# Row tiles over the score buffers, and a projection bias that is added at the zero frequency

## The chip, the cores and the metric

The kernel runs on one core of one Trainium2 chip. The metric is the device time of one execution in microseconds (us). Before the change it is 3673.48 us, the median of three runs (3665.2 to 3677.16).

## The reference

The input `x` is two images of 48 x 48 positions with 768 channels, float32. Two layers follow one another, each added to its own input:

```
def _L0(x):                     # attention over 2304 tokens, 12 heads of 64
    qkv = x.reshape(B, S, dim) @ qkv_w + qkv_b
    attn = (q * scale) @ k.T + rel_h[..., :, None] + rel_w[..., None, :]
    out = softmax(attn) @ v
    return out @ proj_w + proj_b

def _L1(x):                     # a small network per frequency
    xf = rfft2(x, axes=(1, 2), norm='ortho')
    o1 = gelu(block_diagonal(w1) applied to xf + b1)     # complex
    o2 = softshrink(block_diagonal(w2) applied to o1 + b2, 0.01)
    return irfft2(o2, s=(48, 48), norm='ortho')

x = x + _L0(group_norm(x))      # 32 groups
x = x + _L1(group_norm(x))
```

`proj_b` is one value per channel, the same for all 2304 positions of an image. In the transform over both axes such a constant stands at one frequency alone, the zero frequency, where it is 48 times as large.

## The kernel before

The kernel is written with a tile library. Pools of tiles are stacked from the left or from the right end of the on-chip memory; a pool that is opened where another was closed waits for those that used the old one. The library puts each engine's instructions into an order of its own, except those issued through the class `InOrder`: each of these is pinned behind everything already written on its engine. SP issues most transfers, ACT the stores of `y1` and a few at the end of stages.

**Attention** (`attention`) handles both images, 216 units in a row: 12 pairs of heads (`pr`), six groups of 384 queries (`g`), three units of 128 queries each (`x`). A unit's scores stand in one of four buffers `s` of the pool `at_s` (128 partitions, 18,432 bytes each). POOL fills `s` with the position terms; PE adds products, DVE takes the maximum, ACT the exponential, DVE transposes blocks of 32; then `exchange` brings them into `pT` with 12 transfers and 4 copies by ACT; PE (`weigh`, tile `ps_o`) makes the weighted sum two units later. `x` counts units in the loop by `n`; `e` is `n` counted so that the last unit has 17. The results of a unit's group go to DRAM as `oT`, the inverse denominators as `inv_d`; for the last group ACT issues these stores.

**Projection** (`Projection`, `project_out`): 18 row tiles `t` of 128 tokens, in six groups `g` of three. One product (`product`) is 6 matmuls of 384 columns into a bank `acc`; there are two halves `hf` per tile. `parts` loads the tokens of one group in two halves, then `inv_d` in two halves, and has POOL multiply the two. Image 0's projection (`late`) is begun inside attention: `late.early` loads group 0, and at `e` = 11 to 19 nine `late.step()` load the weights (3), the bias (1) and group 1 (4 loads and POOL's product). `late.fill` puts the first six products between the last units. For image 1 `prepare` does the like during the last stages of image 0's spectral part, in a pool `po_r` (`room`).

The sum `x1` (row tile, [128, 24, 768]) holds image rows two by two: partitions 0 to 47 the even one, 64 to 95 and 112 to 127 the odd one. It is allocated after attention, over attention's closed pools. `rows(g)` (L921) loads four pairs of image rows from `x` by SP, three transfers per group, and for image 0 two more that fill the partitions in between (48 to 63, 96 to 111); then POOL adds the bias in four instructions (L930). `outputs` (L963) adds the products into `x1` on DVE, by the pieces that `moves` (L762) yields: 13 for three row tiles and one half. `over_w(n)` (L938) transforms two pairs of rows over the width: eight matmuls `ps_y` over both halves, four copies `y1` by ACT, and two stores `y_d`.

In the loop over `t`, `tokens(g + 1)` and `rows(g + 1)` stand at the first tile of each group.

**Spectral part** (`Spectral`, eight blocks `n` of 96 channels): `load` reads `y_d`; `weights`, `biases` load by SP; `over_h(n)` transforms over the height (`ps_z`, copies by DVE and ACT in turn, squares by ACT); `mean(n)` subtracts the group's mean at the zero frequency (L1092); `norm(n)` makes the group's root from the squares and scales `w1` (L1118), and has POOL add real and imaginary parts into `both`; `first` and `second` are the two layers; `back_h`, `back_w` transform back and add into `x1`, from where the output is stored.

`mean(0)` and `norm(0)` are called from inside `over_h(1)`. PE takes its instructions in order, so the rest of `over_h(1)` stands behind the products in them.

Of the kernel before, what the change touches and what calls it, by code (L numbers as in the profile page):

```python
# [17 lines left out]
P = 128  # L18
# [24 lines left out]
XP = 8  # L43
WP = 5
# [230 lines left out]
def attention(tc, k, xs, a, oTs, inv_ds, late, span, ps_b, ps_o):  # L275
# [12 lines left out]
    with ExitStack() as ctx:  # L288
# [11 lines left out]
        sp = pool("at_s", 4)  # L300
# [362 lines left out]
        for n in range(len(order) + 3):  # L663
# [110 lines left out]


class Projection:


    def __init__(self, tc, k, a, oT, inv_d, span, ps_b, dram, room=None, first=None):
# [5 lines left out]
        if room is not None:  # L785
            shape = [P, self.head + 2 * NCC * UQ]
# [7 lines left out]
        self.steps = [lambda i=i: self.weights(i) for i in range(0, NCC, 2)] + [self.bias]  # L794
# [28 lines left out]
    def pb(self):  # L823
        at = NCC * C if self.room is None else 2 * NCC * UQ
        return self.fixed()[:, at : at + C]
# [14 lines left out]
    def bias(self):  # L840

        src = self.a["proj_b"] if self.k.pb_d is None else self.k.pb_d
        self.nc.sync.dma_start(out=self.pb, in_=src.partition_broadcast(P))

    def values_bias(self, hf):
# [13 lines left out]
        nc.vector.tensor_tensor(self.pb[:, cols], ps[:, :UQ], self.pb[:, cols], ALU.add)  # L859
        if hf:  # L860
            k.pb_d = self.dram.tile([C], F32, tag="pb_d", name="pb_d")
            nc.sync.dma_start(out=k.pb_d, in_=self.pb[0, :])
# [44 lines left out]

def project_out(tc, k, x_b, pr, pools, y_d, x1, constants):
# [9 lines left out]
    x_v = x_b.rearrange("(g k i w) c -> g i w k c", k=4, i=2, w=HW)  # L918
# [12 lines left out]

    rows(0)
# [588 lines left out]
```

## Time and profile before

The profiled execution took 3675.21 us; its span, from first to last instruction, is 3673.4 us, and the 1.8 us beside it lie around the span.

| engine | busy us | share of the span | instructions |
|---|---|---|---|
| PE (matmul) | 3538.6 | 96% | 36416 |
| PEld (weight load, beside PE) | 2447.8 | 67% | 36416 |
| DVE | 2938.3 | 80% | 6867 |
| ACT | 2552.4 | 69% | 3769 |
| POOL | 2045.6 | 56% | 661 |

The stages, read from the chain of waits in order of time:

| stage | from, us | to, us |
|---|---|---|
| attention, both images | 0 | 2846 |
| projection and width of image 0 | 2846 | 3010 |
| spectral part of image 0 | 3010 | 3259 |
| projection and width of image 1 | 3259 | 3424 |
| spectral part of image 1 | 3424 | 3673 |

A busy share is an average over these stages. The chain is followed back from the last instruction, at each step to what released it; it says what the end waited for, stage by stage. "L67" is the line of `InOrder` and stands for every instruction issued through it, so there the tile names tell the groups apart. An instruction's row names the tiles without their numbers: `x` is `x1`, `s` a score buffer, `proj_s` and `proj` the places of the projection of image 0 and 1, `spectrum` all that is cut from one large tile (`z` of even blocks, `d2` and others). SPq and ACTq are the issuing of transfers.

### The profile page before, as it was taken

To read this page: it belongs to the slowest core of one execution; us is meant where nothing else is said; L and a number is where in the kernel's file an instruction comes from. 1 tells how busy PE (TensorE), PEld (TensorE's weight loads), DVE (VectorE), ACT (ScalarE), POOL (GpSimd) and SP (SyncE) were. 2 spreads that over 40 slices of the span, in tenths; PEclk is the share of its full clock that TensorE was granted. 3 is DMA by queue.
4 is the path that set the end of the run, shared out by engine and by line. 5 is a ranking of instruction groups with operands and counts; after the bars stand their busy time and mean duration, and the time that the engine had idled before them with its cause. 6 is when DMAs were issued, how large, how long until landed. Compare 5 with 4: busy or idle time off the path is not lost.

```text
span 3673.4 us, 93676 instructions
## 1 busy us (share of the span) xinstructions
PE 3538.6 (96%) x36416; PEld 2447.8 (67%) x36416; DVE 2938.3 (80%) x6867; ACT 2552.4 (69%) x3769; POOL 2045.6 (56%) x661
## 2 busy tenths in 40 slices
PE   8999999999999999999999999999888799989998
PEld 5676776767767666676776776767666357645665
DVE  4798989998989996799898998989895456645575
ACT  3788888888888887788888888888885024301342
POOL 2566666666665654557576766676673333434232
PEclk9999999999999999999999999999999899999898
DMA  3677777777777885677777777777887775586545
GB/s 105 148 179 172 175 176 175 172 177 173 181 170 178 209 198 118 141 174 180 171 180 167 181 172 175 178 175 172 185 188 164 158 167 116 138 204 163 119 108 140
DMA packets 499085, 608.09 MB, mean 166 GB/s; under 512 B 179249, under 2 KB 311665, under 8 KB 498642
## 3 DMA queue, kind: packets, MB, share of 16 engines
q1 hardware_dynamic: 489692, 585.36, 69.2%
q10 hardware_dynamic: 8950, 16.72, 1.4%
q8 instruction: 289, 4.73, 0.6%
q14 instruction: 154, 1.26, 0.1%
HBM read 133.77 MB, written 85.90 MB: 60 GB/s over the span
## 4 chain that ended last, share of the span: by engine, by line
PE 85%; DMA 5%; DVE 3%; SPq 2%; ACT 1%; issue 1%; POOL 1%; ACTq 0%; DVEq 0%; POOLq 0%
PE ps_o L67 22%; PE ps_s L67 20%; PE ps_proj L67 15%; PE ps_v L67 8%; PE acc L67 7%; PE ps L1206 4%; DVE s L67 2%; PE ps_z L1145 2%; PE ps_u L1245 2%; SPq L67 2%; PE ps_r L67 2%; DMA pT<-s 1%; PE ps_x L67 1%; PE ps_y L67 1%; POOL s L67 1%
## 5 line engine op out<-in xcount | busy, mean ns | idle before, releaser
L67 POOL TENSOR_TENSOR s<-rhw 128x2304 f32<-128x2304 f32 x432 | 1740.6, 4063 | 1032.3 <-DMA pT<-s 559.6
L67 DVE CUSTOM_DVE_ANT_0 s<-ps_s,s 128x512 f32<-128x512 f32 (+1 forms) x2160 | 1222.1, 633 | 308.4 <-issue 224.7
L67 ACT ACTIVATE s<-s,nm 128x1152 f32<-128x1152 f32 x864 | 1074.7, 1245 | 338.1 <-DVE nm L67 331.5
L67 DVE STREAM_TRANSPOSE s<-s 128x1152 f32<-128x1152 f32 x864 | 1111.9, 1344 | 6.0 <-ACT s L67 6.0
L67 ACT COPY pT<-s 32x1152 f32<-32x1152 f32 x864 | 993.6, 1150 | 28.9 <-PE ps_o L67 10.3
L67 PE MATMUL ps_o<-pT,v 128*64 128x128 f32 x15552 | 904.7, 276 | 46.3 <-DMA pT<-s 17.4
L67 PEld LDWEIGHTS ps_o<-pT,v 128*64 128x64 f32 x15552 | 873.3, 139 | 89.4 <-issue 40.5
L67 PE MATMUL ps_s<-kT,qT 64*128 64x512 f32 (+1 forms) x4320 | 902.6, 555 | 6.3 <-ACT xnT L67 2.7
L67 PEld LDWEIGHTS ps_s<-kT,qT 64*128 64x128 f32 x4320 | 432.7, 186 | 421.5 <-issue 345.2
L67 PE MATMUL ps_proj<-xnT,w 128*64 128x384 f32 (+1 forms) x4032 | 592.5, 447 | 4.1 <-ACT xnT L67 2.9
L67 PEld LDWEIGHTS ps_proj<-xnT,w 128*64 128x64 f32 x4032 | 280.4, 138 | 280.0 <-issue 216.8
L969 DVE TENSOR_TENSOR x<-acc,x 32x384 f32<-32x384 f32 (+2 forms) x312 | 173.0, 554 | 189.8 <-PE acc L67 84.5
L67 PE MATMUL ps_v<-w,xnT 128*64 128x128 f32 x5184 | 298.9, 275 | 0.0
L67 PEld LDWEIGHTS ps_v<-w,xnT 128*64 128x64 f32 x5184 | 283.4, 137 | 21.2 <-DVE mx L67 21.2
L956 ACT COPY y<-ps_y 128x384 f32<-128x384 f32 x96 | 40.1, 489 | 318.7 <-PE ps_y L67 290.4
L67 POOL TENSOR_TENSOR spectrum<-spectrum 128x480 f32<-128x480 f32 x80 | 96.2, 1205 | 200.2 <-DVE nm_total L1103 117.4
L67 DVE DVE_READ_ACCUMULATOR2_ANT mx<- 128x1 f32 x2160 | 179.1, 83 | 0.0
L67 ACT ACTIVATION_READ_ACCUMULATOR s<-s,nm 128x1 f32 x864 | 161.2, 187 | 0.0
L1206 PE MATMUL ps<-w,spectrum 96*64 96x96 f32 x3200 | 141.7, 247 | 0.0
L1206 PEld LDWEIGHTS ps<-w,spectrum 96*64 96x64 f32 x3200 | 133.4, 137 | 7.1 <-DVE spectrum L1222 2.9
L67 PE MATMUL acc<-proj_s 128*128 128x384 f32 x360 | 121.5, 496 | 0.1
L67 PEld LDWEIGHTS acc<-proj_s 128*128 128x128 f32 x360 | 68.5, 193 | 53.6 <-issue 8.2
(138 smaller groups left out, 2227.9 us busy)
## 6 DMA issues: line engine op xcount, KB each, us to landing
pT<-s SPq DMA_DIRECT2D x2592, 144.0 KB
t<-rel SPq DMA_DIRECT2D x144, 189.0 KB
rhw<-t SPq DMA_DIRECT2D x144, 144.0 KB
y<-y_d SPq DMA_DIRECT2D x40, 360.0 KB
u_d<-spectrum SPq DMA_DIRECT2D x40, 360.0 KB
u<-u_d SPq DMA_DIRECT2D x48, 300.0 KB
w<-in_qkv_w SPq DMA_DIRECT2D x36, 384.0 KB
oT<-res SPq DMA_DIRECT2D x71, 192.0 KB
```

What stands on the lines that cost most here:

```text
L67: return lambda *args, **kw: self.tc.keep_in_program_order(op(*args, **kw))
L956: nc.scalar.copy(y1[:, i, cols], both[i][:, :UQ])
L969: nc.vector.tensor_tensor(dst, acc[p : p + n, :UQ], dst, ALU.add)
L1145: nc.tensor.matmul(ps[:BS, w * 96 : (w + 1) * 96], lhsT=self.y2[s, j][:, w, i * BS : (i + 1) * BS], rhs=k.fh, start=True, stop=True,)
L1206: nc.tensor.matmul(ps[64 * r : 64 * r + 64, w * BS : (w + 1) * BS], lhsT=self.o1[:, ri, f0 : f0 + 64], rhs=w2[:, (0, 2, 1, 0)[2 * r + ri], ...
L1245: nc.tensor.matmul(ps[: 2 * HW, :480], lhsT=k.ih, rhs=d2[:, c0 : c0 + 480], start=True, stop=True)
```

## The change

- The pool of the score buffers is opened by the caller, at the right end of the memory. At `e` = 18, when the last unit's exchange has been written, `exchanged()` closes it and opens in its place three row tiles `x1[0..2]` of [128, 8, 768] (together as large as the four buffers), and loads the rows of group 0 there: four transfers on SP, ahead of that step's `late.step()`. The fill of partitions 48 to 63 (`BETWEEN`) comes one group later than the rows. After attention, `project_out` no longer loads group 0 for image 0; `fw` is loaded at the very start of the kernel.
- The rows get no bias. `proj_b` is loaded into one partition, `values_bias` makes one row of it, and `pb_d` keeps it in DRAM. Image 1 has no bias step any more, so its nine steps become eight.
- The spectral part of image 0 loads `pb_d` twice (`dc`, a row of 768; `dc_off`, 96 x 8, by single elements), POOL multiplies both by 48, PE and DVE subtract the group's mean. `mean` adds `dc_off` in the same instruction; `second` adds `dc` to the zero frequency's output with one POOL instruction of 1 x 96 per block.
- `over_w` reads 48 partitions of the even row instead of 64, and `moves` yields 14 pieces instead of 13 for three tiles and one half.

```diff
-def attention(tc, k, xs, a, oTs, inv_ds, late, span, ps_b, ps_o):
+def attention(tc, k, xs, a, oTs, inv_ds, late, exchanged, sp, span, ps_b, ps_o):
-        sp = pool("at_s", 4)
...
-            elif 1 < e < 7:
+            elif e == 18:
+                exchanged()
+            if 1 < e < 7:
                 next(late.early)
             elif 11 <= e < 20:
                 late.step()

 def moves(t):
-    done = 0
+    wide = False
     for p in range(0, P, 32):
         k, m = divmod(t % 3 * 4 + p // 32, 3)
-        if p >= done:
-            n = min(P, p + 96 - 32 * m) - p if p in (0, 64) and m == 0 else 32
-            yield p, n, k, 32 * m
-            done = p + n
-        if m == 1:
+        if m == 0:
+            wide = p in (0, 64)
+            yield p, HW if wide else 32, k, 0
+        elif m == 1:
+            if not wide:
+                yield p, HW - 32, k, 32
             yield p, 32, k, 96
+        else:
+            yield p, 32, k, 64

 class Projection:
...
-        self.steps = [lambda i=i: self.weights(i) for i in range(0, NCC, 2)] + [self.bias]
+        self.steps = [lambda i=i: self.weights(i) for i in range(0, NCC, 2)]
+        if k.pb_d is None:
+            self.steps.append(self.bias)
...
     def bias(self):
-        src = self.a["proj_b"] if self.k.pb_d is None else self.k.pb_d
-        self.nc.sync.dma_start(out=self.pb, in_=src.partition_broadcast(P))
+        self.nc.sync.dma_start(out=self.pb, in_=self.a["proj_b"][None, :])

     def values_bias(self, hf):
...
-                ps[:, :UQ],
-                lhsT=k.bv[:, cc : cc + 1].to_broadcast([P, P]),
+                ps[:1, :UQ],
+                lhsT=k.bv[:, cc : cc + 1],

+ROWS = ((0, 0, 0, HW), (64, 1, 0, 32), (112, 1, 32, 16))
+BESIDE = (96, 0, 32, 16)
+BETWEEN = (HW, 1, 32, 16)
+
+def load_rows(sync, x_b, x1, g, places):
+    x_v = x_b.rearrange("(g k i w) c -> g i w k c", k=4, i=2, w=HW)
+    part = x1[g // 2][:, g % 2 * 4 : g % 2 * 4 + 4, :]
+    for q, i, w0, n in places:
+        sync.dma_start(out=part[q : q + n], in_=x_v[g, i, w0 : w0 + n])

     def rows(g):
-        part = x1[:, 4 * g : 4 * g + 4, :]
-        places = [(0, 0, 0, HW), (64, 1, 0, 32), (112, 1, 32, 16)]
-        if pr.room is None:
-            places += [(HW, 1, 32, 16), (96, 0, 32, 16)]
-        for q, i, w0, n in places:
-            pr.sync.dma_start(out=part[q : q + n], in_=x_v[g, i, w0 : w0 + n])
-        for j in range(4):
-            pr.pool.tensor_tensor(part[:, j, :], part[:, j, :], pr.pb, ALU.add)
-
-    rows(0)
+        fresh = pr.room is None
+        load_rows(pr.sync, x_b, x1, g, (*ROWS, BESIDE) if fresh else ROWS)
+        if fresh:
+            load_rows(pr.sync, x_b, x1, g - 1, (BETWEEN,))
+            if g == HW // 8 - 1:
+                load_rows(pr.sync, x_b, x1, g, (BETWEEN,))
+
+    if pr.room is not None:
+        rows(0)
     constants()
     while pr.steps:
         pr.step()
...
-                    r = slice(64 * i, 64 * i + 64)
+                    r = slice(64 * i, 64 * i + (64 if i else HW))

 class Spectral:
+    def constants_at_zero(self):
+        nc, k = self.nc, self.k
+        if k.dc is not None:
+            return
+        k.dc = self.small.tile([1, C], F32, tag="dc", name="dc")
+        k.dc_off = self.small.tile([BS, NBK], F32, tag="dc_off", name="dc_off")
+        self.sync.dma_start(out=k.dc, in_=k.pb_d[None, :])
+        with nc.allow_non_contiguous_dma(reason="biases onto partitions"):
+            self.sync.dma_start(out=k.dc_off, in_=k.pb_d.rearrange("(n o) -> o n", o=BS))
+        self.pool.tensor_scalar(k.dc, k.dc, float(HW), 0.0, ALU.mult, ALU.add)
+        self.pool.tensor_scalar(k.dc_off, k.dc_off, float(HW), 0.0, ALU.mult, ALU.add)
+
+    def offsets_at_zero(self):
+        nc, off = self.nc, self.k.dc_off
+        mean = self.bank("ps_nm")
+        nc.tensor.matmul(mean[:BS, :NBK], lhsT=self.k.gmean, rhs=off, start=True, stop=True)
+        nc.vector.tensor_tensor(off, off, mean[:BS, :NBK], ALU.subtract)

     def mean(self, n):
...
-        nc.vector.tensor_tensor(z0, z0, mean[:BS, :1], ALU.subtract)
+        nc.vector.scalar_tensor_tensor(
+            z0, z0, self.k.dc_off[:, n : n + 1], mean[:BS, :1], ALU.add, ALU.subtract
+        )

     def second(self, n, ahead):
...
             self.pool.tensor_tensor(val, val, clip, ALU.subtract)
+            if j == 0:
+                dc = self.d2[:1, 0, i * BS : (i + 1) * BS]
+                self.pool.tensor_tensor(dc, dc, k.dc[:, n * BS : (n + 1) * BS], ALU.add)

     def run(self):
...
         self.biases()
+        fresh = k.dc is None
+        self.constants_at_zero()
         over_h(0)
+        if fresh:
+            self.offsets_at_zero()

 def block_kernel(tc, a, out):
-        k.load(nc.sync, a, cp, {"rel": [P, 2 * REL]})
+        k.load(nc.sync, a, cp, {"rel": [P, 2 * REL], "fw": [P, 64]})
...
+        s_rooms, x1 = ExitStack(), [None] * 3
+        in_order = InOrder(tc, nc.sync)
+
+        def exchanged():
+            s_rooms.close()
+            x_pool = ctx.enter_context(tc.tile_pool(name="sp_x", bufs=1, side="right"))
+            for j in X1_ORDER:
+                x1[j] = x_pool.tile([P, XP, C], F32, tag=f"x1_{j}", name=f"x1_{j}")
+            load_rows(in_order, a["x"][0], x1, 0, (*ROWS, BESIDE))
+
+        sp = s_rooms.enter_context(tc.tile_pool(name="at_s", bufs=4, side="right"))
+        attention(tc, k, a["x"], a, oTs, inv_ds, late, exchanged, sp, span, ps_b, ps_o)
```

Every other use of `x1` (`over_w`, `outputs`, `back_w` and its stores) picks the tile and the row in it; `X1_ORDER` is (1, 0, 2).

More of the change, by code (lines that the diff above doesn't have):

```diff
@@ L43 @@
 XP = 8
+X1_ORDER = (1, 0, 2)
 WP = 5
@@ L785, in __init__ @@
         if room is not None:
-            shape = [P, self.head + 2 * NCC * UQ]
+            shape = [P, NCC * C + 2 * NCC * UQ]
             self.room = room.tile(shape, F32, tag="proj", name="proj")
@@ L823, in pb @@
     def pb(self):
-        at = NCC * C if self.room is None else 2 * NCC * UQ
-        return self.fixed()[:, at : at + C]
+        return self.spans()[:1, NCC * C : NCC * C + C]
     def weights(self, c0):
@@ L858, in values_bias @@
             )
-        nc.vector.tensor_tensor(self.pb[:, cols], ps[:, :UQ], self.pb[:, cols], ALU.add)
+        nc.vector.tensor_tensor(self.pb[:, cols], ps[:1, :UQ], self.pb[:, cols], ALU.add)
         if hf:
             k.pb_d = self.dram.tile([C], F32, tag="pb_d", name="pb_d")
-            nc.sync.dma_start(out=k.pb_d, in_=self.pb[0, :])
+            nc.sync.dma_start(out=k.pb_d[None, :], in_=self.pb)
     def product(self, t, hf):
@@ L917, in project_out @@
     bank = lambda name: ps_b.tile([P, 512], F32, tag="b", name=name)
-    x_v = x_b.rearrange("(g k i w) c -> g i w k c", k=4, i=2, w=HW)
     y_v = y_d.rearrange("(q i) t c -> t q i c", i=2)
     def rows(g):
-        part = x1[:, 4 * g : 4 * g + 4, :]
-        places = [(0, 0, 0, HW), (64, 1, 0, 32), (112, 1, 32, 16)]
-        if pr.room is None:
-            places += [(HW, 1, 32, 16), (96, 0, 32, 16)]
-        for q, i, w0, n in places:
-            pr.sync.dma_start(out=part[q : q + n], in_=x_v[g, i, w0 : w0 + n])
-        for j in range(4):
-            pr.pool.tensor_tensor(part[:, j, :], part[:, j, :], pr.pb, ALU.add)
-    rows(0)
+        fresh = pr.room is None
[6 more added lines that the diff above has]
+        rows(0)
     constants()
@@ L949, in over_w @@
                         lhsT=k.fw[r, :],
-                        rhs=x1[r, 2 * n + c, cols],
+                        rhs=x1[n // 4][r, 2 * (n % 4) + c, cols],
                         start=True,
@@ L967, in outputs @@
         for p, n, j, q in moves(t):
-            dst = x1[q : q + n, t // 3 * 4 + j, cols]
+            dst = x1[t // 6][q : q + n, t // 3 % 2 * 4 + j, cols]
             nc.vector.tensor_tensor(dst, acc[p : p + n, :UQ], dst, ALU.add)
@@ L1189, in second @@
     def second(self, n, ahead):
-        nc = self.nc
+        nc, k = self.nc, self.k
         s, i = divmod(n, NB)
@@ L1286, in back_w @@
                 for m in range(2):
-                    t0 = j * XP + m * XP // 2 + t
-                    dst = self.x1[:, t0 : t0 + 2, ch]
+                    t0 = m * XP // 2 + t
+                    dst = self.x1[j][:, t0 : t0 + 2, ch]
                     self.nc.vector.tensor_tensor(
@@ L1292, in back_w @@
             ts = slice(j * XP, (j + 1) * XP)
-            for q, i, w0, n in ((0, 0, 0, HW), (64, 1, 0, 32), (112, 1, 32, 16)):
+            for q, i, w0, n in ROWS:
                 queue = self.nc.scalar if last and i else self.sync
                 queue.dma_start(
-                    out=self.out_v[i, w0 : w0 + n, ts, ch], in_=self.x1[q : q + n, ts, ch]
+                    out=self.out_v[i, w0 : w0 + n, ts, ch], in_=self.x1[j][q : q + n, :, ch]
                 )
     def run(self):
+        k = self.k
         pieces = list(range(KW // WP))
@@ L1354, in block_kernel @@
         nc.gpsimd.memset(k.eps, GN_EPS)
-        k.load(nc.sync, a, cp, {"rel": [P, 2 * REL]})
-        k.pb_d = None
+        k.load(nc.sync, a, cp, {"rel": [P, 2 * REL], "fw": [P, 64]})
+        k.pb_d = k.dc = None
         k.bv = cp.tile([P, NCC], F32, tag="bv", name="bv")
@@ L1391, in prepare @@
                 ready[-1].fill(2)
-        attention(tc, k, a["x"], a, oTs, inv_ds, late, span, ps_b, ps_o)
+        s_rooms, x1 = ExitStack(), [None] * 3
[8 more added lines that the diff above has]
+        attention(tc, k, a["x"], a, oTs, inv_ds, late, exchanged, sp, span, ps_b, ps_o)
         small = ctx.enter_context(tc.tile_pool(name="sp_small", bufs=1))
-        x_pool = ctx.enter_context(tc.tile_pool(name="sp_x", bufs=1))
-        x1 = x_pool.tile([P, HW // 2, C], F32, tag="x1", name="x1")
-        fourier = {"fh": [96, 96], "fw": [P, 64], "ih": [P, 96], "iw": [P, 2, 64], "gmean": [BS, BS]}
+        fourier = {"fh": [96, 96], "ih": [P, 96], "iw": [P, 2, 64], "gmean": [BS, BS]}
         def constants():
             if fourier:
-                k.load(InOrder(tc, nc.sync), a, small, fourier)
+                k.load(in_order, a, small, fourier)
                 fourier.clear()
```

## The prediction

> **What bounds the kernel now.** I read the chain of waits first, by engine and then by line: PE holds 85% of it, so what is not PE work on that chain is all that can be won without touching the products.
>
> ```profile
> PE 85%; DMA 5%; DVE 3%; SPq 2%; ACT 1%; issue 1%; POOL 1%; ACTq 0%; DVEq 0%; POOLq 0%
> ```
>
> Then the same chain in order of time where attention ends and the projection of image 0 begins (start, length, what; x counts instructions):
>
> ```profile
> 2842.24 4.10 PE ps_o L67 x72
> ...
> 2851.06 1.82 DMA inv_d<-turned
> ...
> 2853.02 6.07 DMA x<-in_x
> ...
> 2859.11 6.69 DMA iw<-in_iw
> 2865.80 3.55 POOL x L67 x2
> ...
> 2872.36 5.47 PE ps_y L67 x12
> 2877.83 10.18 PE acc L67 x24
> 2888.01 1.45 PE ps_y L67 x16
> ```
>
> The last weighted sum ends at 2846.3 and the first new product starts at 2877.8. In between PE needs only one `over_w`, 1.45 us elsewhere, so 30 us are lost: the row loads wait until attention's last store has landed, then come 12.8 us of landing (2853.0 to 2865.8), POOL's bias adds, and DVE's adds that free PSUM. From there PE is unbroken: the stage table (us, then busy time of PE, PEld, DVE, ACT, POOL, granted clock, DMA share, GB/s) has it at 128.32 of 128.40.
>
> ```profile
> 2846.30:2877.80 31.50, 8.75 (x20) 2.08 (x18) 9.26 (x17) 1.96 (x5) 7.68 (x5) 0.58 0.81 132
> 2877.80:3006.20 128.40, 128.32 (x497) 69.17 (x496) 70.67 (x129) 16.07 (x39) 55.25 (x24) 0.98 0.75 169
> 3259.40:3286.40 27.00, 21.17 (x67) 10.67 (x65) 12.91 (x24) 1.92 (x4) 12.14 (x5) 0.94 1.05 213
> ```
>
> Last I read SP's timeline, for when a load could go out, and POOL's, for the start of the spectral part:
>
> ```profile
> 2822.18 3.80 SPq L67 DMA_DIRECT2D pT<-s  x6
> 2826.02 0.62 SPq L67 DMA_DIRECT2D proj_s<-inv_d  x1
> 2853.02 2.24 SPq L67 DMA_DIRECT2D x<-in_x  x5
> ...
> 3022.63 3.17 SPq L67 DMA_DIRECT2D b<-in_b  x4
> ```
>
> ```profile
> 3271.56 7.09 POOL L67 TENSOR_TENSOR x<-x,proj 128x768 f32<-128x768 f32 x4 [35.77 <-DMA x<-in_x]
> 3281.26 5.05 POOL L67 TENSOR_TENSOR proj_s<-proj_s,proj 128x2304 f32<-128x2304 f32 x1 [2.60 <-DMA proj<-inv_d]
> ```
>
> **Term 1, rows loaded from inside attention: -24 us.** The rows of group 0 now lie on the score buffers, and those are read last by the six `pT<-s` issued 2822.18 to 2825.98. So the loads can be issued at 2826.0 at best. The worst case comes from the DMA table in steps of 5 us: share 1.07 for 2825 to 2830, 0.63 for 2830 to 2835, 0.00 for 2835 to 2840. All that was in flight, with 576 KB of `inv_d` that now comes later, had landed before 2835; 2833 is the latest. I take 2830.5. Landing takes the 12.8 us of before (four loads instead of five, on a queue that is otherwise idle, so rather less): 2843, between 2839 and 2846. DVE starts then, since POOL's adds are gone. The first `over_w` needs the row tiles t = 0 and 1 added in both halves: by `moves` now 2 x (4 + 5) = 18 adds instead of 16, at a spacing of 0.572 us (five take 2.86), 10.3 us. With the last pair of `ps_y`, 0.75 us, the products restart at 2854 instead of 2877.8: -24. Bounds: -28 with the early issue, -21 with the late one.
>
> This wait is new on SP. Behind it in that queue stand the second half of `inv_d` (group 1), the constants, the rows of group 1 and the tokens of group 2. The half of `inv_d` used to be issued at 2826.02 and POOL's product began at 2834.08, 8 us later. Issued at 2832.5 it lands at 2840.5, at 2847 behind all the rows; with POOL's 5.07 us group 1 is ready at 2846 to 2852, just ahead of 2854. The tokens of group 2 are needed one group later (26.4 us in steady state) and keep their distance from the rows of group 0.
>
> The restart stays slow: the granted clock was 0.50 from 2855 to 2880, and the first 24 products took 10.18 us instead of 7.94. I leave that 2.2 us in. The Trainium skill, TensorE: Matmul & The Clock Gate, section Why this matters for your kernels, says that one idle window of about 3 us puts PE back to half clock; PE still idles from 2846.5 to about 2850, so by it too nothing of this comes back. Were there no idle time, the total would be some 2 us lower.
>
> **Term 2, bias at the zero frequency: +6 us, once.** `constants_at_zero` issues two loads from SP behind `biases`, whose four end at 3025.80. The loads go out by 3026.8 (0.5 us each, the median of `b<-in_b`). The second is 768 single elements. Nothing in the trace shows its landing alone. Nearest below: POOL scaled `w` 1.7 us after the last `w<-in_w` had been issued (3020.50 to 3022.20). Nearest above: `b1`, twice the same pattern, was in use at 3038.29, at most 12 us after the last bias issue. I take 5 us, since it lies behind 384 KB of `b2` on a queue at a share of 0.99 (3020 to 3040): 3032. Then POOL's two scalings (0.35 us for 192 columns; the 768 of `dc` can go first), PE's `ps_nm` 0.25, DVE's subtraction 0.15: 3033. Only now can `mean(0)` go, which ran at 3023.80. After it come the square of 0.55, the total 0.16, `ps_nv` 0.30 and the 5.4 us from 3029.22 to the first product at 3034.63: 3039.8, 5 us late, and 1 more for PE's clock after the stall. Bounds 0 (landed by 3027, since the squares held the total until 3028.4 anyway) and 12.
>
> Who queues there: on PE the offsets' product stands ahead of `over_h(1)`, on DVE `mean(0)` ahead of the copies of `z`, on POOL the scalings ahead of the `both` adds (3.01 us) that the first product reads. They wait for the same landing, not one after another.
>
> The Trainium skill, DMA: Bandwidth & Descriptors, section Rules for kernel authors, speaks against this load: a non-contiguous last dimension becomes one descriptor per element, and it says to rearrange. Its section on latency puts a round trip to memory at some 0.8 us at the least; with that alone this term would be an estimated 1 us and the total 3649. No row of before shows one such load alone.
>
> **Term 3, start of image 1: -3 us.** PE waited for group 1 (POOL `proj_s`, 3281.26 to 3286.31), that for `inv_d`, and DVE for POOL's bias adds. Without the bias step one half of group 1's tokens (576 KB) moves into the earlier `prepare`; at 213 GB/s that is 2.8 us less ahead of `inv_d`. DVE would start at 3271.5 and free the banks at 3271.5 + 10.3 + 0.75 = 3282.6, so POOL, at 3283.5, decides: -3. Bounds 0 (the landing has other causes) and -5 (POOL early, DVE decides).
>
> **Small terms.** `fw` is loaded at the very start, ahead of the first `x`: one issue, 0.46 us, on the path: +0.5 (0 to 0.5). `ps_y` reads 48 rows instead of 64 in one half. Nearest row: `ps_x` with 50 rows has a median of 533 ns against 482, minimum 482 for both. All of it would be 0.15 us on each of 24 `over_w`, 3.6; I take 0.5.
>
> At nothing: the other 44 of the 48 POOL adds (1.81 us each, 85 in all), hidden under PE. 24 more DVE adds at 0.554, 13.3 us, hidden since DVE is busy 70.67 of 128.40; 13.3 if that cover went. 16 POOL adds of 1x96 between 0.10 (a memset of one column) and 0.35 us, at most 5.6, under PE in stages where POOL is busy a third of the time. `values_bias` keeps its 7.94 us, as its moving columns are the same. The two bias broadcasts of 384 KB less are 2 us of DMA each at 195 GB/s, where no wait of the chain ended on them.
>
> **Sum.** -24 + 6 - 3 + 0.5 + 0.5 = -20. The profiled execution took 3675.2 (span 3673.4), which gives 3655.2. It is 1.7 above the median of 3673.5, which gives 3653.5. I say 3654.
>
> **Rivals.** (A) The rows stay behind the end of attention, because reuse of memory waits for more than the score buffers. For it: SP's wait before 2853.02 ended on attention's stores. Against it: there the one `x1` tile lay over all of attention's pools, now only over one. Rows at 2853.0, landed at 2865.8, product at 2876.9: -1 - 3 + 7 makes 3677. (B) The zero-frequency load lands at its upper bound and the rows late: +12, -21, -3 and 1: 3663. (C) Slower: 48 rows no longer run beside the 64 of the other half. Now eight products of `ps_y` take 1.45 us where a whole-array product takes 0.66 (7.94 for twelve); with halves one after another, eight take 2.65, +1.2 on each of 24 `over_w`, +29, and 3683. It outweighs the rest from 0.85 us per `over_w`. Against it: 24 products of `ps_x` with 50 rows take 5.72 us, 0.24 each, far from 0.66. (D) Rows land by 2839, dc by 3029 and image 1 gains its 5: -28 + 2 - 5 + 1: 3644.
>
> **How the numbers follow.** Forecast 0.68, A 0.08, B 0.11, C 0.06, D 0.07. A measurement of this kernel tells about 0.3% (11 us) from no change, so under 3662.5 is faster and over 3684.5 slower. Faster: 0.65 of the forecast, D, and 0.05 of B, 0.77. Within: A, 0.06 of B and 0.01 of C, 0.15. Slower: 0.05 of C, and 0.03 of the forecast for a wait that no row shows, 0.08. The range 3644 to 3670 takes in D and B and leaves out A and C.
>
> **What would show it.** Right: `x<-in_x` issued near 2830, no POOL row `x<-x`, `acc` restarting near 2854, and the part between 3020 and 3040 stretched by some 6 us with a wait of POOL or PE on the new tile. Wrong: SP idle until attention's stores (A), `acc` waiting for POOL `proj_s` near 2854, no gap at the zero frequency, `ps_y` over 1.9 us per `over_w` (C).

## The result and the profile after

The changed kernel takes 3680.82 us (median of 20 runs, 3672.95 to 3687.14) against 3673.76 of the kernel before, run beside it (20 runs, 3665.2 to 3677.16): a ratio of 1.0019, interval 1.0012 to 1.0026. Measured twice more in later series it had ratios of 1.0017 (1.0008 to 1.0026) and 1.0010 (1.0000 to 1.0019). It is slower by 3 to 7 us in the three series (in the last one the interval reaches 1), where 20 us less were forecast.

The profiled execution of the changed kernel took 3673.48 us (span 3671.7), 7.3 less than the median. So the two profiles shown are not compared by their spans, but stage by stage, and both kernels were profiled twice more. By the profiled executions alone the changed kernel would be the shorter one, by 1.9 us in the mean of three (3673.7 against 3675.6). Lines of the program shift: attention's helper is L68 now, the row adds L986, the `over_h` products L1185, the first layer L1220.

The chain of waits by engine (page, part 4) has a little more PE and a little less DMA than before, the same share of POOL, and says little:

```profile
PE 87%; DMA 4%; DVE 3%; SPq 2%; issue 2%; ACT 1%; POOL 1%; ACTq 0%; DVEq 0%; POOLq 0%
```

Three places say more. First the restart of the products, in the same chain in order of time (start, length, what):

```profile
2837.85 4.11 PE ps_o L68 x72
...
2842.27 1.88 DMA oT<-res
...
2844.16 5.78 DMA proj_s<-inv_d
...
2850.15 5.04 POOL proj_s L68
...
2855.24 10.12 PE acc L68 x24
```

and SP's timeline beside it (start, length, transfer, count):

```profile
2826.89 8.12 SPq L68 DMA_DIRECT2D x<-in_x  x4
2844.16 0.63 SPq L68 DMA_DIRECT2D proj_s<-inv_d  x1
2844.88 12.45 SPq L68 DMA_DIRECT2D x<-in_x  x5
```

The rows went out at 2826.9, earlier than forecast, and DVE's row adds began at 2833.3. But the second half of `inv_d` for group 1 was issued only at 2844.16, in the moment in which attention's last `oT` store had landed; then came its landing, POOL's product, and the first `acc` at 2855.24. From the last `ps_o` (2841.9) to there it is 13.3 us, against 31.4 before.

Second the zero frequency, in PE's timeline (in brackets the idle time just before, and what ended it):

```profile
3002.36 1.09 PE L1185 MATMUL ps_z<-fh,y 96*96 96x96 f32 x10 [0.32 <-DMA y<-y_d]
3009.98 0.49 PE L1097 MATMUL ps_nm<-dc_off,gmean 96*96 96x8 f32 x2 [6.53 <-POOL dc_off L68]
...
3021.68 1.62 PE L1220 MATMUL ps<-both,w 96*96 96x400 f32 x2 [2.26 <-POOL w L1108]
```

PE waits 6.53 us for POOL's scaling of `dc_off`. Third the end of image 0's spectral part, SP and then PE:

```profile
3218.79 11.29 SPq L1292 DMA_DIRECT2D u_d<-spectrum  x5
3232.86 0.38 SPq L68 DMA_DIRECT2D proj_s<-oT  x1
3233.29 8.97 SPq L68 DMA_DIRECT2D out<-x  x9
3242.31 4.72 SPq L68 DMA_DIRECT2D u<-u_d  x6
```

```profile
3228.40 7.90 PE L68 MATMUL acc<-proj 128*128 128x384 f32 x24
3247.37 1.51 PE L68 MATMUL ps_x<-u,iw 50*64 50x384 f32 x2 [11.07 <-DMA u<-u_d]
```

`u_d` has been written by 3232.7, but the loads of `u` go out at 3242.3, behind one half of group 1's tokens of image 1 and nine stores. The same place in the profile of before, SP and then PE:

```profile
3219.42 8.93 SPq L67 DMA_DIRECT2D out<-x  x9
3228.46 11.13 SPq L1249 DMA_DIRECT2D u_d<-spectrum  x5
3242.38 4.79 SPq L67 DMA_DIRECT2D u<-u_d  x6
```

```profile
3237.88 7.90 PE L67 MATMUL acc<-proj 128*128 128x384 f32 x24
3247.64 0.83 PE L67 MATMUL ps_x<-u,iw 50*64 50x384 f32 x2 [1.85 <-DMA u<-u_d]
```

There the loads went out at 3242.38 too, but right behind the writes of `u_d`, which ended at 3242.2. The head start of 9.5 us that was left here (`acc` at 3228.40 against 3237.88) is gone after this wait.

The same in a stage table of the changed kernel (us, then busy time of PE, PEld, DVE, ACT, POOL, granted clock as a share of full TensorE speed, DMA share, GB/s): restart, projection, way to the layers, and the wait of the last fence.

```profile
2841.90:2855.20 13.30, 3.80 (x19) 0.95 (x17) 7.77 (x14) 2.24 (x6) 5.03 (x1) 0.65 0.75 135
2855.20:2994.70 139.50, 137.57 (x524) 74.16 (x528) 74.82 (x135) 16.46 (x40) 20.23 (x4) 0.98 0.73 170
2994.70:3021.70 27.00, 17.65 (x125) 14.84 (x125) 10.33 (x30) 11.96 (x33) 7.94 (x15) 0.71 1.04 215
3228.00:3247.40 19.40, 8.33 (x27) 4.61 (x25) 0.65 (x1) 0.55 (x1) 0.00 (x0) 0.77 0.74 194
```

The second row is the fourth place: the projection itself is no longer unbroken (137.57 of 139.50 busy, against 128.32 of 128.40 in the row of before).

From such profiles every run below is read by four distances, in us: **restart** (end of the last `ps_o` to the first `acc`), **projection** (first to end of the last `acc` of image 0), **to layers** (to the first `ps_1r`, the third matmul instruction of the first layer, 1.4 us behind its first), **rest** (from there to PE's last product). Their sum is set against the mean of the three profiles of before, and beside it stand the medians of the timed runs.

| kernel | restart | projection | to layers | rest | sum against before | median against before | ratio (interval) |
|---|---|---|---|---|---|---|---|
| before, 3 profiles | 31.4, 32.3, 31.8 | 136.5, 135.7, 136.3 | 21.8, 22.4, 22.0 | 631.3, 633.3, 631.5 | 0 | 0 | 1 |
| changed, 3 profiles | 13.3, 13.1, 13.0 | 139.5, 140.9, 141.3 | 28.4, 27.8, 27.6 | 642.2, 642.9, 642.8 | +2.2 | +7.1, +4.2, +3.0 | 1.0019, 1.0017, 1.0010 |
| e1 three steps | 13.1 | 142.8 | 28.2 | 630.7 | -7.3 | -4.1 | 0.9987 (0.9977 to 0.9996) |
| e2 inv first | 14.4 | 152.0 | 28.6 | 637.5 | +10.4 | +8.8 | 1.0029 (1.0017 to 1.0041) |
| e3 dc early | 13.1 | 148.6 | 22.1 | 643.3 | +5.0 | +0.9 | 1.0003 (0.9994 to 1.0012) |
| e4 three steps, dc late | 13.1 | 142.9 | 22.0 | 633.9 | -10.2 | -11.1 | 0.9971 (0.9960 to 0.9982) |
| e5 inv by POOL | 7.5 | 142.2 | 21.2 | 636.6 | -14.6 | -15.5 | 0.9964 (0.9952 to 0.9975) |
| e6 rows late | 27.1 | 140.2 | 29.8 | 644.3 | +19.3 | +17.0 | 1.0046 (1.0033 to 1.0059) |
| e7 rows first | 7.5 | 148.5 | 22.1 | 637.1 | -6.9 | -7.7 | 0.9973 (0.9964 to 0.9983) |
| e8 between by POOL, twice | 7.5, 7.5 | 141.3, 142.6 | 21.8, 22.1 | 631.7, 635.0 | -19.8, -14.9 | -18.1, -11.5 | 0.9950 (0.9938 to 0.9962), 0.9964 (0.9950 to 0.9977) |
| e9 old adds | 8.5 | 141.0 | 21.3 | 636.8 | -14.5 | -14.5 | 0.9961 (0.9949 to 0.9973) |

The sums follow the medians within 5 us over a range of some 35, so the four distances hold nearly all of what the change does.

### The profile page after: what moved, and what is told of

Same layout as the page of the kernel before. It is cut to its first block, busy times and chain, and to the rows that moved or that the text cites. A ratio compares the mean times of both kernels' runs of the same rounds, so it can differ in the third digit from the quotient of the medians.

```text
span 3671.7 us, 93628 instructions
## 1 busy us (share of the span) xinstructions
PE 3536.5 (96%) x36418; PEld 2447.5 (67%) x36418; DVE 2954.7 (80%) x6892; ACT 2551.4 (69%) x3769; POOL 1966.3 (54%) x631
## 4 chain that ended last, share of the span: by engine, by line
PE 87%; DMA 4%; DVE 3%; SPq 2%; issue 2%; ACT 1%; POOL 1%; ACTq 0%; DVEq 0%; POOLq 0%
PE ps_o L68 22%; PE ps_s L68 20%; PE ps_proj L68 15%; PE ps_v L68 8%; PE acc L68 8%; PE ps L1246 3%; SPq L68 2%; DVE s L68 2%; PE ps_z L1185 2%; DMA pT<-s 2%; PE ps_u L1288 2%; PE ps_r L68 2%; PE ps_x L68 1%; PE ps L1220 1%; PE ps_y L68 1%
## 5 line engine op out<-in xcount | busy, mean ns | idle before, releaser
L68 POOL TENSOR_TENSOR s<-rhw 128x2304 f32<-128x2304 f32 x432 | 1740.1, 4060 | 1031.7 <-DMA pT<-s 599.9
L68 DVE CUSTOM_DVE_ANT_0 s<-ps_s,s 128x512 f32<-128x512 f32 (+1 forms) x2160 | 1222.1, 633 | 305.8 <-issue 206.4
L68 ACT ACTIVATE s<-s,nm 128x1152 f32<-128x1152 f32 x864 | 1074.6, 1245 | 340.3 <-DVE nm L68 334.5
L68 DVE STREAM_TRANSPOSE s<-s 128x1152 f32<-128x1152 f32 x864 | 1112.0, 1344 | 6.0 <-ACT s L68 6.0
L68 ACT COPY pT<-s 32x1152 f32<-32x1152 f32 x864 | 993.4, 1150 | 27.3 <-PE ps_o L68 8.9
L68 PE MATMUL ps_o<-pT,v 128*64 128x128 f32 x15552 | 902.5, 275 | 44.8 <-ACT res L68 18.3
L68 PEld LDWEIGHTS ps_o<-pT,v 128*64 128x64 f32 x15552 | 871.4, 139 | 87.5 <-issue 48.8
L68 PE MATMUL ps_s<-kT,qT 64*128 64x512 f32 (+1 forms) x4320 | 901.2, 555 | 6.9 <-ACT xnT L68 3.3
L68 PEld LDWEIGHTS ps_s<-kT,qT 64*128 64x128 f32 x4320 | 432.8, 186 | 421.0 <-issue 344.1
L68 PE MATMUL ps_proj<-xnT,w 128*64 128x384 f32 (+1 forms) x4032 | 592.2, 447 | 4.1 <-ACT xnT L68 2.9
L68 PEld LDWEIGHTS ps_proj<-xnT,w 128*64 128x64 f32 x4032 | 280.7, 138 | 279.1 <-issue 216.4
L986 DVE TENSOR_TENSOR x<-acc,x 32x384 f32<-32x384 f32 (+2 forms) x336 | 186.0, 554 | 161.2 <-PE acc L68 132.2
L68 PE MATMUL ps_v<-w,xnT 128*64 128x128 f32 x5184 | 298.9, 275 | 0.0
L68 PEld LDWEIGHTS ps_v<-w,xnT 128*64 128x64 f32 x5184 | 283.4, 137 | 21.2 <-DVE mx L68 21.2
L68 POOL TENSOR_TENSOR spectrum<-spectrum 128x480 f32<-128x480 f32 x80 | 96.2, 1204 | 201.5 <-DVE spectrum L1262 193.8
L68 DVE DVE_READ_ACCUMULATOR2_ANT mx<- 128x1 f32 x2160 | 178.8, 83 | 0.0
L68 ACT ACTIVATION_READ_ACCUMULATOR s<-s,nm 128x1 f32 x864 | 161.3, 187 | 0.0
L68 PE MATMUL acc<-proj_s 128*128 128x384 f32 x360 | 121.4, 496 | 5.7 <-POOL proj_s L68 5.7
L68 PEld LDWEIGHTS acc<-proj_s 128*128 128x128 f32 x360 | 68.5, 193 | 59.1 <-POOL proj_s L68 7.0
```

Of the source, the lines that this page charges most:

```text
L68: return lambda *args, **kw: self.tc.keep_in_program_order(op(*args, **kw))
L986: nc.vector.tensor_tensor(dst, acc[p : p + n, :UQ], dst, ALU.add)
```

## The experiments

**Second and third profiles.** The changed kernel and the kernel before, unaltered, because one profile of each could not explain the medians.

> The changed kernel once more, unaltered, to have a second profile. Theory 1 (attention's length wanders from run to run by some us, and the first profile of the changed kernel caught a short one): the median is again near 3681 (ratio to before 1.001 to 1.003), the last ps_o ends 4 to 9 us later than the 2841.9 of the first profile, and the distances behind it stay (13.3 us from there to the first acc, 166 us from that to the first product of the layers, an 11 us wait of PE ahead of the ps_x near 3247). Rival: what is missing lies behind attention: the last ps_o is again near 2842 and one of those distances is longer by several us.

> The changed kernel a third time, for more times and a third profile. Theory (its profiles so far were short executions of it): the median is again 5 to 8 us over that of the kernel before, ratio 1.001 to 1.003, the distances behind attention are those of the two profiles within 2 us (restart 13, first acc to first layer product 168, from there to the end 642), and the last ps_o ends 2 to 6 us later than the 2841 of those two if this execution is near the median. Rival (the profiles are typical, and the times wander): the median is within 3 us of before.

> The kernel before, once more, to have a second profile of it. Theory (the first profile of it caught a long attention): the last ps_o ends near 2840 to 2842 instead of 2846.3, as in five profiles of changed kernels, and the distances behind it are those of the first profile within 1 us (31.4 to the first acc, 136.5 to the last, 21.8 to the first layer product). Rival (the changed kernels have a shorter attention, by the score buffers on the other side or the early fw): it ends near 2846 again.

> The kernel before a third time, for a third profile. Theory (attention's length wanders by some us whatever the kernel): the last ps_o ends anywhere between 2840 and 2846, and the distances behind it stay (32, 158, 632). Rival (the changed kernels' attention is about 4 us shorter): it ends at 2844 or later, as in the two profiles so far, and that of the changed kernel near 2841.

Medians: the changed kernel 3676.53 (ratio 1.0017) and 3676.11 (1.0010), the single runs of before 3676.34 and 3675.3. The distances behind attention stayed, as expected. The theory that attention's length wanders whatever the kernel did not hold: the last `ps_o` ended at 2841.9, 2840.4 and 2841.8 in the changed kernel, at 2846.3, 2844.3 and 2845.3 before, 3.9 us apart in the mean. The timed runs of the changed kernel show no such gain, since its sums without it already lie below its medians. What makes the difference in profiled executions stays open; it decides nothing below, where the end of attention is the zero.

**e1, the fourth step of the early preparation.**

```
-                    for _ in range(4):
+                    for _ in range(3):
                         pr.step()
```

> The changed kernel, but image 1's early preparation takes three steps instead of four, so that no load into the spectrum's memory stands in SP's queue ahead of nine output stores and the u loads. Theory (the queue is held): the nine stores go out near 3219 again, the six u loads as soon as u_d has been written (3233 instead of 3242), PE's wait of 11.1 us ahead of ps_x becomes under 2 us, and the kernel is 8 to 10 us faster than the changed one: near 3672, ratio to before 0.998 to 1.000. Rival (the start of image 1 waits for something else anyway, for example its late accs or the row adds of DVE): the u loads go out early, but the first acc of image 1 stays where it was against the end, and the time stays near 3681.

Measured: 3668.19 us, 8.3 under the changed kernel of the same series. SP and PE at the same place:

```profile
3209.76 8.31 SPq L68 DMA_DIRECT2D out<-x  x9
3219.45 11.36 SPq L1292 DMA_DIRECT2D u_d<-spectrum  x5
3233.58 4.80 SPq L68 DMA_DIRECT2D u<-u_d  x6
```

```profile
3238.22 0.83 PE L68 MATMUL ps_x<-u,iw 50*64 50x384 f32 x2 [1.27 <-DMA u<-u_d]
3239.89 3.16 PE L68 MATMUL ps_x<-u,iw 50*64 50x384 f32 x16 [0.84 <-DMA u<-u_d]
```

The nine stores are out before the writes of `u_d` begin, the loads follow these at once, and the wait of 11.07 us has become 2.1 in two pieces. From the first `acc` of image 1 to the first `ps_x` it is 9.2 us here, 19.0 in the changed kernel (3228.40 to 3247.37) and 9.8 before (3237.88 to 3247.64). The same distance is 18.3 to 19.0 in all six profiles with four steps, 9.0 to 9.8 in all seven with three and 9.0 to 9.8 in the three of before: that one load held the queue, for 9.3 us in the mean. The rest of the kernel is 11.9 us shorter (642.6 to 630.7) and the median 8.3; so closely the rest can't be read, since it lies between 630.7 and 637.1 in the profiles with three steps and between 637.5 and 644.3 in those with four.

**e2, the half of `inv_d` ahead of the rows.**

```
-            elif e == 18:
-                exchanged()
             if 1 < e < 7:
                 next(late.early)
             elif 11 <= e < 20:
                 late.step()
+            if e == 18:
+                exchanged()
```

> The changed kernel, but the second half of inv_d for group 1 is issued ahead of the four row loads of group 0 instead of behind them. Theory (that half set the restart: it was issued at 2844.2, 18 us later than before, behind rows and a counter raised by attention's last store): it goes out near 2822, POOL's product of group 1 is done before 2846, and then DVE's row adds decide; the first acc restarts 8 to 9 us behind the last ps_o instead of 13.3, and the kernel is 4 to 5 us faster than the changed one: near 3676. Rival (DVE's adds or the ps_y banks set the restart as much): the half is early and acc restarts within 1 us of 13.3.

Measured: 3681.09 us, 4.6 over the changed kernel of the same series, and neither theory's number. SP's timeline, then the chain of waits at the restart:

```profile
2821.61 0.62 SPq L68 DMA_DIRECT2D proj_s<-inv_d  x1
2827.16 17.31 SPq L68 DMA_DIRECT2D x<-in_x  x4
```

```profile
2842.26 1.89 DMA oT<-res
...
2844.16 3.66 DMA x<-in_x
```

The half went out at 2821.6 as wanted, but now the four row loads were issued over 17.31 us: the last of them went out at 2844.16, when attention's last store had landed. The wait had moved from one load to the other. The built program shows why, and the trace, which names for each transfer the counter that it raises and the last one that it waits for, agrees. Transfers of SP and ACT take eight completion counters (0 to 7 here) in turn, in the order in which they were scheduled over both queues, and a transfer first waits until the last one on its counter has landed. In the changed kernel (transfer, time of issue, counters):

```
SP   2834.69  x<-in_x (fourth row load)   waits for counter 1, raises 1
ACT  2842.27  oT<-res                     raises counter 2 (landed 2844.15)
SP   2844.16  proj_s<-inv_d               waits for counter 2, raises 2
```

The half of `inv_d` reads nothing of that store. It stands behind it because both have counter 2, and in e2 it is the fourth row load that has the store's counter (6 there). The third and fourth row load in turn wait for the counters of the first and second, which is why four issues took 8.12 us in the changed kernel. In this run PE also waited 6.62 us for POOL `proj_s` in the middle of the projection, which is part of its 152.0.

**e3, the bias loads into the projection.** `constants_at_zero` becomes a function called in `project_out`:

```
             pr.tokens(g + 1)
             rows(g + 1)
+            if g == 3:
+                at_zero()
```

> The changed kernel, but the two loads of the bias at the zero frequency and their scaling by POOL are put into the projection of image 0 (its fourth group) instead of behind the bias loads of the spectral part. Theory (that landing costs some 6 us ahead of the first mean): PE's wait for POOL dc_off is gone, the first product of the layers comes 160 to 161 us behind the first acc of the restart instead of 166.4, and the kernel is 5 to 6 us faster than the changed one: near 3675. Rival (the 9.6 us lost between restart and first layer product come from the end of the projection: row loads issued over 24 us, and y landing later): the wait for dc_off goes, the distance stays above 164.

Measured: 3673.21 us, 3.3 under the changed kernel of the same series. The wait for `dc_off` was gone and the way to the layers 22.1 us, as before the change; but the projection grew to 148.6, since the two `inv_d` loads behind `dc_off` were issued over 9.86 us and an `acc` waited 2.75 us for POOL `proj_s`. The landing is worth what the theory said; the place gave half of it back.

**e4, both repairs, the loads at a better place.** As e1 and e3, with `g == 4`: behind the last row loads.

> Three steps in image 1's early preparation, and the two loads of the bias at the zero frequency issued behind the last row loads of image 0's projection, where SP has nothing to do for some 20 us (2970 to 2992). In the run that put them behind the fourth group, the first product of the layers came 22.1 us behind the last acc instead of 27.8, but the projection itself took 148.6 us instead of 140.9, with SP's inv_d loads behind dc_off issued over 9.9 us instead of 1.3. Theory (the loads were put at a bad place; the landing itself is worth 6 us): the last acc to the first layer product 22 us, first to last acc 140 to 143 us, and about 6 us faster than with three steps alone: near 3662, ratio to before 0.996 to 0.998. Rival (768 single elements slow the projection wherever they are, or the first mean then waits for something else): the sum of both distances stays near 169 and the time near 3668.

Measured: 3663.33 us, ratio 0.9971, and 22.0 and 142.9 us: as the theory had it.

**e5, the half of `inv_d` on POOL's queue.** Its transfers have counters of their own: the trace of this run has a ninth one, for POOL's.

```
+            queue = self.pool if g == h == 1 and self.room is None else self.sync
-            self.sync.dma_start(
+            queue.dma_start(
                 out=inv[h * HD : (h + 1) * HD],
```

> The kernel with three steps and late dc loads, and the second half of inv_d for group 1 of image 0 issued on POOL's own queue instead of SP's, where in the built program it waits for the completion counter that attention's last oT store raises. Theory (that half, and it alone, sets the restart): POOL's product of group 1 is done before 2842, the restart comes 7.5 to 9 us behind the last ps_o instead of 13.1, when the last ps_y has been done, and the kernel is 4 to 6 us faster than the one before it: near 3657. Rival (DVE's row adds or the landing of the rows come next within 1 us): the restart stays at 12 us or more and the time near 3662.

Measured: 3658.9 us, 4.4 under e4 of the same series. POOL's product of group 1, and then PE at the restart:

```profile
2823.49 5.06 POOL L68 TENSOR_TENSOR proj_s<-proj_s 128x2304 f32<-128x2304 f32 x1 [37.78 <-DMA proj_s<-inv_d]
```

```profile
2848.57 1.55 PE L68 MATMUL ps_y<-x,fw 64*64 64x384 f32 x6 [2.92 <-ACT y L974]
2850.05 10.34 PE L68 MATMUL acc<-proj_s 128*128 128x384 f32 x24
```

Group 1 is ready 20 us before it is needed, and the restart comes 7.5 us behind the last `ps_o`. What decides now is a copy of ACT that stands behind five issues of `inv_d<-turned` on its queue, 0.73 to 1.34 us each.

**e6, the rows behind attention again.** `exchanged()` is called behind `attention`, and its pool lies on the left.

```
-            elif e == 18:
-                exchanged()
...
+        exchanged()
-            x_pool = ctx.enter_context(tc.tile_pool(name="sp_x", bufs=1, side="right"))
+            x_pool = ctx.enter_context(tc.tile_pool(name="sp_x", bufs=1))
```

> The changed kernel with its row tiles back on the left, over attention's other pools, and loaded behind attention, as the kernel before does it; the bias at the zero frequency and the 48 rows stay. It prices the two halves of the change. Theory (the rows are worth some 15 us, the bias costs): restart 26 to 29 us behind the last ps_o, 6 us more than before from the last acc to the first layer product, the 11 us wait ahead of the last ps_x but one still there, and the kernel is 13 to 17 us slower than the changed one: near 3692, ratio to before 1.004 to 1.006. Rival (the early rows are what stretches the projection and holds the queue, by moving all loads against each other): less than 8 us slower than the changed one, near 3683.

Measured: 3691.42 us, ratio 1.0046. The early rows are worth 27.1 - 13.1 = 14.0 us at the restart. What is left of the change saves 31.8 - 27.1 = 4.7 there, without POOL's bias adds, and is still 17 us slower than before by the medians, 19 by the sum: 12.3 of it in the rest (644.3, SP's queue), 7.7 in the way to the layers (29.8), 4.0 in the projection. So the longer projection (140.2) is there without the early rows too.

**e7 and e8, the longer projection.** e7 swaps `rows(g + 1)` and `pr.tokens(g + 1)` in e5; e8 puts the loads of `BETWEEN` in e5 on POOL's queue.

```
-            load_rows(pr.sync, x_b, x1, g - 1, (BETWEEN,))
+            load_rows(pr.pool, x_b, x1, g - 1, (BETWEEN,))
```

> The fastest kernel so far (three steps, late dc loads, inv_d half on POOL's queue), with the row loads of each group issued ahead of that group's tokens and inv_d instead of behind them. It is about the 6 us by which the projection itself is longer than before (142 us from first to last acc against 136). Theory (the last group's rows land so late that DVE's adds and with them the last but one ps_y wait, 1.6 us idle near 2975 and a slow clock behind it): rows of the last group issued by 2955, no idle time there, first to last acc 137 to 139 us, and 3 to 5 us faster: near 3655. Rival (the tokens now stand behind the rows, and POOL's product of a group comes late): acc waits for POOL proj_s once or more, and the kernel is no faster or up to 8 us slower: 3659 to 3667.

> The fastest kernel so far, with the six loads of the rows between (16 partitions that only have to hold something) on POOL's queue, so that SP issues four row loads a group, as few as the rows need. Theory (the sixth and fifth load, each behind the completion counters of older transfers, make the last rows late): the last group's row loads are issued over 16 us or less instead of 23, first to last acc 137 to 139 us instead of 142, and 3 to 5 us faster: near 3655. Rival (the number of adds on DVE sets the end of the projection, 4.5 adds for a half tile instead of 4): first to last acc stays at 141 to 143 and the time near 3659.

> The kernel with six loads on POOL's queue once more, beside the next one on the same chip: 3655 again within 4 us, ratio to before 0.994 to 0.996, first to last acc 141 to 142 us with PE idle near the last but one ps_y (2.2 us in the first profile of it).

Measured: e7 3665.45 us, e8 3655.06 and 3659.6. In e7 each side was right in part. The rival: an `acc` waited 10.34 us for POOL `proj_s`. The theory: the idle time of PE near the end is gone, and the last sixth of the projection (60 instructions of `acc`) takes 21.6 us, as in all three profiles of before, while it takes 25.7 to 28.8 in every other profile of the changed kernel and of its variants. In e8 the last row loads were issued over 13.9 us and long before they were needed, but the projection stayed at 141.3 and 142.6: the late loads are not its cause. Whether e8 is faster than e5 isn't settled (ratios 0.9950 and 0.9964 against 0.9964).

**e9, fewer adds.** e8 with `moves` of the kernel before; `BETWEEN` is loaded with its own group, since the wide add writes over it. A group then has 26 adds on DVE instead of 28 (by `moves`, 2 x 13 and 2 x 14; the 24 and 30 of the expectation are wrong).

> The same kernel with the adds of the kernel before: one of 96 partitions instead of one of 48 and one or two more, so that a group has 24 adds on DVE and not 30; the rows between are loaded for each group with its rows, still on POOL's queue, since such an add writes over them. Theory (the larger number of adds, taken at nothing in the forecast, sets the end of the projection): first to last acc 136 to 138 us instead of 141.3, no idle time of PE above 1 us between the restart and the last acc, and 3 to 5 us faster than the kernel beside it: near 3651. Rival (the order in which the adds of the last group are worked, or the load on the queues, does it): first to last acc stays at 140 or more and the times agree within 2 us.

Measured: 3656.63 us beside 3659.6 for e8, intervals overlapping; projection 141.0. The rival was right about the projection. DVE near the end of the projection, in e9 and then in the kernel before:

```profile
2966.98 0.55 DVE L982 TENSOR_TENSOR x<-acc,x 96x384 f32<-96x384 f32 x1 [2.69 <-PE acc L68]
2972.50 0.55 DVE L982 TENSOR_TENSOR x<-acc,x 32x384 f32<-32x384 f32 x1 [4.96 <-PE acc L68]
2976.37 6.35 DVE L982 TENSOR_TENSOR x<-acc,x 32x384 f32<-32x384 f32 x11 [3.32 <-PE acc L68]
```

```profile
2977.92 2.87 DVE L969 TENSOR_TENSOR x<-acc,x 32x384 f32<-32x384 f32 x5 [1.01 <-PE acc L67]
2981.79 2.86 DVE L969 TENSOR_TENSOR x<-acc,x 32x384 f32<-32x384 f32 x5 [1.00 <-PE acc L67]
```

Before, DVE adds five pieces behind each half product, a microsecond after the last five. In e9 it makes one add, waits for a later product, makes one more, waits, and then has eleven at once (twelve in the others, but for e7); meanwhile PE stands (start, length, product, idle time before):

```profile
2976.26 0.86 PE L68 MATMUL ps_y<-x,fw 48*64 48x384 f32 x2
2978.73 1.40 PE L68 MATMUL ps_y<-x,fw 64*64 64x384 f32 x4 [1.62 <-issue]
...
2981.21 5.83 PE L68 MATMUL acc<-proj_s 128*128 128x384 f32 x12
```

The twelve matmul instructions behind it (one product) take 5.83 us instead of 4.14 elsewhere. And e7, with 28 adds a group, has the order of before near the end:

```profile
2961.84 2.87 DVE L987 TENSOR_TENSOR x<-acc,x 16x384 f32<-16x384 f32 x5 [1.01 <-PE acc L68]
2965.71 2.83 DVE L987 TENSOR_TENSOR x<-acc,x 32x384 f32<-32x384 f32 x5 [1.00 <-PE acc L68]
```

So it goes with the order in which DVE takes the adds, not with their number or with the late loads: with the order of before the last sixth has its old length (e7), with the other one it is 4 to 7 us longer. Why the order comes out differently, and came out as before when the rows were issued ahead of the tokens, stays open, and no variant on record has the old order without a wait for POOL.

## Why the prediction was wrong

By its own terms, forecast and measured (means of three profiles each): the rows -24 and -18.7; the bias at the zero frequency +6 and +5.9; the start of image 1 -3 and +10.6; the projection, taken at nothing, +4.4. The sum is +2.2 instead of -20.

- **Term 3 failed, and it is the largest miss** (+10.6 in the rest instead of -3). The prediction said that without the bias step "one half of group 1's tokens (576 KB) moves into the earlier `prepare`" and counted only its bytes. It did not ask where that load writes. Its destination lies in the tile that the spectrum still uses, so it waits for the last work on the spectrum, and nine stores and six loads stand behind it on a queue kept in order: 9.3 us more at PE, all of which e1 gets back by taking that one step away. The gain of 3 itself did not come either: from the first `ps_x` to the first `acc` of group 1 it is 38.9 us in the changed kernel and 38.1 in e1, against 38.7, 37.3 and 38.1 before. The forecast had POOL decide; POOL was ready at 3284.5, but the chain goes over DVE's adds up to 3284.8 and the last `ps_y`. The prediction did name what queues behind a new wait in terms 1 and 2; for a step that moves forward because another one vanishes it did not.
- **Term 1 was right about the rows and wrong about `inv_d`.** Rows issued at 2826.9 (forecast 2830.5, bounds 2826 and 2833), DVE's adds from 2833.3 (forecast 2843): better than forecast. The step that failed is "group 1 is ready at 2846 to 2852, just ahead of 2854". The half was issued not right behind the rows, the last of which left SP at 2835.0, but 9 us later still, since it had the same completion counter as a store of ACT that it doesn't depend on. e5 moves it to another queue: the restart comes 24.3 us earlier than before (7.5 against 31.8). That this is the -24 of the forecast is chance: the forecast ended on DVE's adds from 2843 on, in e5 they began at 2833.6 and ACT's copy decided.
- **Term 2 was right in cause and size, the size in part by luck:** 5.9 on the way to the layers, and e4 gets them back by issuing the loads earlier, while SP is idle. The landing was shorter than the 5 us taken, 3.12 in the chain, and came 15.0 us behind the last `acc`, where the forecast had 17.8; but from it to the first layer product it was 12.0 us instead of 8.8, partly since 20 instructions of `ps_z` stood on PE ahead of `ps_nv` (1.7 us), and the granted clock was 0.71 in this stage. SP issued the load only at 3006.54, because the bias loads ahead of it waited for the counters of two stores of ACT (the chain has `y_d<-y` up to 3004.14, then SP): the like of the wait in term 1. The Trainium skill, DMA: Bandwidth & Descriptors, section Rules for kernel authors, speaks against the element-wise load `dc_off`; here it landed in 3.12 us where its contiguous neighbour `dc` was in use 2.40 us after its issue, so by this one pair its pattern costs an estimated 0.7 us, and its place in the queue the rest.
- **"24 more DVE adds ... hidden" was right about the adds and wrong about the stage.** DVE had the time (74.82 of 139.50 us busy), and e7 and e9 show that the number isn't it; but the adds are worked in another order, and PE waits at the end: +4.4 where the prediction has nothing. (The POOL adds taken at nothing are 80 us, 44 of 1.81, not 85; nothing hangs on it.)
- **Rivals.** A (rows behind attention) did not happen; e6 makes it and takes 3691, not 3677, because the queue of term 3 and the longer projection are in it. C (48 rows lose concurrency) is refuted: sixteen `ps_y` instructions take 1.45 us as before; nothing of the 0.5 us taken for them as a gain is seen either. B did not come: the rows went out early and not late, and the load at the zero frequency landed sooner than taken. What did come of the waits named ahead is `acc` waiting for POOL `proj_s`, which stands under the signs of being wrong. No rival ended on the slower side by the mechanism that did it.
- The restart stayed slow, as said: the granted clock was 0.65 from 2841.9 to 2855.2 and the first 24 instructions of `acc` (two products; the prediction calls them 24 products) took 10.12 us. The new wait shows the like: behind the 11.07 us of idle time the granted clock was 0.50 from 3249.3 to 3258.6, and the 48 instructions of `acc` from 3258.66 took 17.51 us. Before, where PE had waited 1.85 and 1.09 us at this place, the clock was 0.64 (3247.6 to 3259.3) and they took 16.57; in steady state they take 15.75. For the 11.07 us this agrees with the rule of the Trainium skill, TensorE: Matmul & The Clock Gate, section Why this matters for your kernels, that an idle window of about 3 us puts PE back to half clock. The clock of before fell here too, behind waits that are each shorter than that.

## What to carry to other kernels

When a step is taken out of a list that is worked through by count, every later step moves up by one: look at what it writes and who still uses that memory, and at what is queued behind it. When a load is put ahead of others on a queue, look at the built program for the counters that each transfer waits for: a load can stand behind a store that it has nothing to do with, and a change of order only hands that wait to its neighbour (e2), while another queue ends it (e5). The change with these three places mended (e5 and e8) takes 3655 to 3660 us, 11 to 18 less than before, where 20 were forecast: more than half of it was there, and was given back in waits that the shares of busy time do not show.

## What the runs showed of the hardware that was not expected

- The time of one kernel goes with its mean granted clock from run to run, though not strictly: among the 20 runs of the changed kernel the fastest, 3672.95 us, had 0.977, the slowest, 3687.14, had 0.972.
- Transfers on POOL's queue went out without regard to the waits of SP and ACT: with the half of `inv_d` there, POOL's product was done at 2828.6, against 2855.2.
- In e5 each issue of the five small stores `inv_d<-turned` (1.5 to 3 KB) held ACT for 0.73 to 1.34 us, the issue of the 192 KB store `oT<-res` ahead of them for 0.36; behind the five a copy came so late that PE stood 2.92 us ahead of the last `ps_y`.
